# Graph attention with one leading neighbour: where the products of W stand among the projections

## The chip, the cores and the metric

The kernel runs on one core of a Trainium2 chip. The metric is the device time of one execution in microseconds (us), the median of several runs. Its engines are named as the profile names them: PE (TensorE matmul), PEld (its weight loads), DVE (VectorE), ACT (ScalarE), POOL (GpSimd) and SP (SyncE, which here only issues transfers). Each takes its instructions in the order in which the program gives them.

## The reference

The computation is one graph attention layer with four heads, a residual and a layer norm. x is 4096x512, adj 4096x4096, W 512x2048 (four heads of 512 columns) and a 4x1024x1, all float32.

```
ht = (h @ W).reshape(N, N_HEADS, N_HIDDEN).transpose(1, 0, 2)
src = jnp.einsum('hnd,hd->hn', ht, a[:, :N_HIDDEN, 0])
dst = jnp.einsum('hnd,hd->hn', ht, a[:, N_HIDDEN:, 0])
e = leaky_relu(src[:, :, None] + dst[:, None, :], 0.01) + adj_mat[None]
att = softmax(e, axis=-1)
h_prime = einsum('hij,hjd->hid', att, ht)
x = _layernorm(x + h_prime.mean(axis=0), axis=-1)
```

The adjacency holds weights of up to 1e9 and is added to scores of ordinary size. In a row whose largest adjacency entry leads the second by more than the scores can make up, the softmax is 1 at that column and 0 elsewhere. Then the layer gives x[i] + x[col(i)] @ mean over heads of W, followed by the norm.

## The kernel before, in words

`leading_rows` computes this short form for all rows, and a bound that tells whether it holds. `general`, the full attention, follows only where the bound fails; with the inputs here it does not run. So all that is profiled is `leading_rows`, lines 66 to 369.

The 4096 rows are worked in 32 blocks of 128 rows. The loop variable t counts 32 steps, and each step works on several blocks at different stages:

- **Adjacency.** SP loads a block of adj (128x4096, 2 MB) into one of six buffers; step t issues the load of block t+5, so the load waits until the block that used the buffer has been reduced. x is loaded in eight groups of four blocks into the tile `hold`, at steps given by the table `x_at`. W is first held in the slots of `hold` that the last four groups of x take over later, so those loads also wait for the products that read W.
- **Search.** DVE takes the maxima of segments of 64 columns in two halves (`segment_maxima(t, 0)` and `(t, 1)`, line 151). `find_segment(t)` finds the best segment and POOL gathers it from memory (`lead`, line 166). Two steps later `find_column(t-2)` finds the column in it, between the two halves, and POOL gathers that row of x (`y`, line 182; four buffers).
- **Projection.** At step t `project(t-3)` opens a sum in PSUM (`o`) with the residual, as identity times the block of x (line 191), turns y by four transposes into `tp` (line 194), has ACT copy them to `yt` (line 196), and adds four products of yt with `w_sum`, the mean of W over heads (line 198).
- **Norm.** `stats(t-4)` has ACT sum o and its squares (lines 208 and 210). At each even step from 6 on, `rstd` turns the sums of blocks t-6 and t-5 into scale and shift: a square root on ACT (line 213), then a reciprocal and a product on DVE (lines 214 and 215). `finish` applies them on ACT (line 219).
- **Bound.** It needs the products of W with both halves of a: W has sixteen 128x512 pieces, and `head_vector(kb, h)` turns one by four transposes (line 255), copies it on ACT (line 257) and forms four narrow products, two columns wide, into `pv` (line 259). The table `vectors_at` gives the steps: four pieces each at steps 1 and 2, one each at steps 3 to 10. `head_norms` follows at step 11. `row_norm` sums squares of x on ACT, and `bound` puts it together in three parts at steps 27 to 29.

After the loop come the last two columns, the last pairs' norms, the stores of the output by SP, `test` (the check of the bound, with one product on PE at line 307) and the projections of blocks 29 to 31. The order on every engine is the order of these calls, written by hand. In float32 the profile shows each matmul as two instructions, so four products of 512 columns are listed as x8.

Of the kernel before, what the change touches and what calls it, by code (L numbers as in the profile page):

```python
# [9 lines left out]
F32 = mybir.dt.float32  # L10
# [9 lines left out]
P = 128  # L20
# [45 lines left out]
def leading_rows(ctx, tc, x, adj, W, a, out, ident, v, n_bad, any_bad):  # L66
# [91 lines left out]
    def find_segment(ib):  # L158
        seg = seg_of.pop(ib)
        nc.vector.max(out=top[:, ib, :], in_=seg)  # L160
        at = small.tile([P, 8], U32, name="at")
        nc.vector.max_index(at, top[:, ib, :], seg)
        row = small.tile([P, 1], U32, name="row")
        nc.vector.tensor_tensor(row, at[:, 0:1], first[:, ib : ib + 1], op=OP.add)  # L164
        lead = small.tile([P, E], F32, name="lead")
        nc.gpsimd.indirect_dma_start(  # L166
            out=lead, out_offset=None, in_=adj_segs,
            in_offset=bass.IndirectOffsetOnAxis(ap=row[:, :1], axis=0),
        )
        at_of[ib], lead_of[ib] = at, lead  # L170
# [14 lines left out]
        )  # L185
        y_t[ib] = y

    def project(ib):
        y = y_t.pop(ib)
        o = psum.tile([P, D], F32, name="o")  # L190
        nc.tensor.matmul(o, ident, hold[:, ib, :], start=True, stop=False)  # L191
        tp = psum.tile([P, KB, P], F32, name="tp", bufs=2)
        for kb in range(KB):
            nc.tensor.transpose(tp[:, kb, :], y[:, ts(kb, P)], ident)  # L194
        yt = rows.tile([P, KB, P], F32, name="yt")
        nc.scalar.copy(yt, tp)  # L196
        for kb in range(KB):
            nc.tensor.matmul(o, yt[:, kb, :], w_sum[:, kb, :], start=False, stop=(kb == KB - 1))  # L198
        o_ps[ib] = o

    def row_norm(ib):
        sq = rows.tile([P, D], F32, name="sq")
# [9 lines left out]
    def rstd(i):  # L212
        nc.scalar.activation(sd[:, i], sd[:, i], AF.Sqrt, bias=eps, scale=1.0 / D)  # L213
        nc.vector.reciprocal(sd[:, i], sd[:, i])  # L214
        nc.vector.tensor_mul(nm[:, i], nm[:, i], sd[:, i])  # L215
# [35 lines left out]
    def head_vector(kb, h):  # L251

        tp = psum.tile([P, KB, P], F32, name="tp", bufs=2)
        for k in range(KB):
            nc.tensor.transpose(tp[:, k, :], hold[:, w_at + kb * H + h, ts(k, P)], ident)  # L255
        wt = rows.tile([P, KB, P], F32, name="wt")
        nc.scalar.copy(wt, tp)  # L257
        for k in range(KB):
            nc.tensor.matmul(  # L259
                pv[:, kb, h : 2 * H : H], wt[:, k, :], at_d[:, k, h : 2 * H : H],  # L260
                start=(k == 0), stop=(k == KB - 1),
            )

    def head_norms():
        nc.vector.tensor_copy(v, pv)
        vv = once.tile([P, KB, 2 * H], F32, name="vv")
        nc.vector.tensor_mul(vv, v, v)
        pn = psum.tile([P, KB, 2 * H], F32, name="px", bufs=1)
        nc.tensor.matmul(pn, ones, vv, start=True, stop=True)
        n2 = once.tile([P, 2 * H], F32, name="n2")  # L270
        nc.vector.tensor_reduce(n2, pn.rearrange("p k c -> p c k"), axis=AX.X, op=OP.add)
        nc.scalar.activation(n2, n2, AF.Sqrt)
        both = once.tile([P, H], F32, name="both")
        nc.vector.tensor_add(both, n2[:, :H], n2[:, H:])
        nc.vector.tensor_reduce(vn, both, axis=AX.X, op=OP.max)
# [34 lines left out]
        nc.vector.tensor_reduce(total, pg, axis=AX.X, op=OP.add)  # L310
        nc.vector.tensor_scalar(any_bad, total, -1.0, float(N), op0=OP.mult, op1=OP.add)

    x_at = {1: 1, 3: 2, 6: 3, 12: 4, 14: 5, 17: 6, 20: 7}
    norms_at = {t: [t - 2] for t in range(2, 18)}
    for k in range(8):
        norms_at[18 + k] = [16 + 2 * k, 17 + 2 * k]
    vectors = [(kb, h) for kb in range(KB) for h in range(H)]
    vectors_at = {1: 4, 2: 4, **{t: 1 for t in range(3, 11)}}
    COLUMN, PROJECT, STATS, FINISH = 2, 3, 4, 6

    for t in range(NB):
        if t in x_at:
            load_x(x_at[t])
        load_adj(t + AHEAD)
        segment_maxima(t, 0)
        if t >= COLUMN:
            find_column(t - COLUMN)
        if t >= FINISH and t % 2 == 0:
# [9 lines left out]
        if t == 11:  # L338
            head_norms()
        if t >= PROJECT:  # L340
            project(t - PROJECT)
        if t >= FINISH and t % 2 == 0:
# [6 lines left out]
        if 27 <= t <= 29:  # L349
            bound(t - 27)  # L350

    find_column(NB - 2)
    find_column(NB - 1)
# [246 lines left out]
```

## Time and profile before

| | us |
|---|---|
| median of 3 runs (lowest, highest) | 283.46 (280.98, 283.83) |
| the profiled execution | 282.4 |
| its span, first to last instruction | 280.5 |
| PE busy | 220.3 (79%) |
| DVE busy | 192.1 (68%) |
| ACT busy | 120.7 (43%) |
| POOL busy | 61.8 (22%) |

The kernel moves 97.75 MB, 89.15 read and 8.39 written, at a mean of 348 GB/s over the span. The mean granted clock of TensorE is 0.921 of full speed. The profiled execution took 1.9 us more than its span, which is what lies around the first and last instruction. A share of busy time is an average over stages with different limits, so the stages are read apart below: by slices of the span, by who waited for whom, and by the order of time. In the rows of a timeline the first number is the start in us from the start of the span, the second the length; what stands in brackets at the end is how long the engine was idle before it and who released it. In rows of the chain of work that ended last, the name is followed by xcount.

### The profile page before, as it was taken

What the parts mean: (1) busy time and instruction counts of PE and PEld (TensorE: products, weight loads), DVE (VectorE), ACT (ScalarE), POOL (GpSimd) and SP (SyncE); (2) the same over time, 40 slices, a digit from 0 to 9 for tenths busy, and PEclk for the clock granted to TensorE, in tenths of its full rate; (3) what the DMA queues carried; (4) which work ended last, traced back from release to release, by engine and by line L of the source; (5) the groups of instructions that cost most, each with busy time, mean ns of one, the idle gap of its engine ahead of it and who ended that gap; (6) DMA issues with size and microseconds to landing.
All of it is one profiled execution on the core that took longest, in us unless ns stands there. A gap on an engine that the chain in (4) does not pass through costs nothing.

```text
span 280.5 us, 2442 instructions
## 1 busy us (share of the span) xinstructions
PE 220.3 (79%) x683; PEld 112.6 (40%) x684; DVE 192.1 (68%) x381; ACT 120.7 (43%) x295; POOL 61.8 (22%) x75
## 2 busy tenths in 40 slices
PE   0389877778888888889987879887999789888980
PEld 0134666654444444434433333433444334343430
DVE  2524878840029695888999999599879999983011
ACT  1010211211465455365453735674566434465540
POOL 1101123310002222122332332232322322232000
PEclk9999755559999999999999997999899979999997
DMA  7999999999999979499999999999999999415121
GB/s 232 436 416 425 418 425 393 430 400 435 430 409 402 388 289 408 154 416 409 409 426 421 408 418 426 407 418 428 420 355 361 329 408 407 152 42 162 67 101 59
DMA packets 18147, 97.75 MB, mean 348 GB/s; under 512 B 1992, under 2 KB 1992, under 8 KB 13776
## 3 DMA queue, kind: packets, MB, share of 16 engines
q1 hardware_dynamic: 14384, 87.82, 77.9%
q0 software_dynamic: 3584, 9.44, 9.2%
q10 hardware_dynamic: 160, 0.28, 0.3%
q8 instruction: 7, 0.11, 0.2%
q14 instruction: 12, 0.10, 0.1%
HBM read 89.15 MB, written 8.39 MB: 348 GB/s over the span
## 4 chain that ended last, share of the span: by engine, by line
PE 43%; DMA 19%; DVE 18%; ACT 12%; issue 5%; ACTq 0%; POOLq 0%
PE o L198 19%; DVE seg L151 13%; DMA y<-in_x_dram,col 11%; PE pv L259 8%; DMA hold<-in_L_gnn_W_dram 6%; PE o L191 5%; ACT yt L196 4%; PE tp L255 4%; PE tp L194 3%; ACT wt L257 3%; PE o L238 3%; ACT sq L210 2%; DMA adj_t<-in_adj_dram 2%; ACT sq L203 2%; ACT sq L208 1%
## 5 line engine op out<-in xcount | busy, mean ns | idle before, releaser
L151 DVE TENSOR_REDUCE seg<-adj_t 128x32 f32<-128x2048 f32 (+1 forms) x68 | 146.2, 2153 | 22.9 <-DMA adj_t<-in_adj_dram 22.8
L198 PE MATMUL o<-w_sum,yt 128*128 128x512 f32 x256 | 123.4, 627 | 21.6 <-ACT yt L196 21.6
L198 PEld LDWEIGHTS o<-w_sum,yt 128*128 128x128 f32 x256 | 47.8, 197 | 78.5 <-issue 49.1
L196 ACT COPY yt<-tp 128x512 f32<-128x512 f32 x32 | 18.7, 585 | 86.0 <-PE tp L194 86.0
L166 POOL DMA_INDIRECT lead<-in_adj_dram,row x32 | 30.3, 948 | 107.8 <-DVE row L164 99.7
L182 POOL DMA_INDIRECT y<-in_x_dram,col x32 | 30.2, 944 | 85.7 <-issue 62.7
L214 DVE RECIPROCAL sd<-sd 128x2 f32<-128x2 f32 (+1 forms) x17 | 2.8, 163 | 48.7 <-ACT sd L213 48.6
L191 PE MATMUL o<-hold,ident 128*128 128x512 f32 x64 | 34.6, 623 | 0.0
L259 PE MATMUL pv<-at_d,wt 128*128 128x2 f32 x128 | 23.4, 304 | 11.3 <-ACT wt L257 11.3
L259 PEld LDWEIGHTS pv<-at_d,wt 128*128 128x128 f32 x128 | 22.0, 259 | 16.3 <-ACT wt L257 16.3
L238 PE MATMUL o<-hold,ident 128*128 128x512 f32 x32 | 15.6, 646 | 13.1 <-DMA hold<-in_L_gnn_W_dram 13.1
L194 PEld LDWEIGHTS tp<-ident,y 128*128 128x128 f32 x128 | 15.8, 143 | 25.2 <-issue 25.0
L194 PE MATMUL tp<-ident,y 128*128 128x128 f32 x128 | 19.9, 279 | 5.9 <-DMA y<-in_x_dram,col 5.9
L257 ACT COPY wt<-tp 128x512 f32<-128x512 f32 x16 | 9.4, 586 | 34.6 <-PE tp L255 34.6
L219 ACT ACTIVATE hold<-o,nm,sd 128x512 f32<-128x512 f32 x31 | 22.7, 780 | 3.0 <-DVE nm L215 3.0
L210 ACT ACTIVATE sq<-o,nm 128x512 f32<-128x512 f32 x31 | 21.3, 687 | 1.0
L203 ACT ACTIVATE sq<-hold 128x512 f32<-128x512 f32 x32 | 19.7, 619 | 0.0
L208 ACT ACTIVATE sq<-o 128x512 f32<-128x512 f32 x31 | 18.7, 603 | 0.0
L191 PEld LDWEIGHTS o<-hold,ident 128*128 128x128 f32 x64 | 11.5, 195 | 10.0 <-issue 9.9
L238 PEld LDWEIGHTS o<-hold,ident 128*128 128x128 f32 x32 | 6.5, 209 | 21.1 <-issue 18.9
L255 PE MATMUL tp<-ident,hold 128*128 128x128 f32 x64 | 13.3, 346 | 0.0
L239 ACT ACTIVATE w_sum<-o 128x512 f32<-128x512 f32 x4 | 2.4, 597 | 24.1 <-PE o L238 24.1
(66 smaller groups left out, 94.3 us busy)
## 6 DMA issues: line engine op xcount, KB each, us to landing
adj_t<-in_adj_dram SPq DMA_DIRECT2D x30, 2048.0 KB, 12.0
hold<-in_x_dram SPq DMA_DIRECT2D x8, 1024.0 KB, 15.8
out_dram<-hold SPq DMA_DIRECT2D x7, 1024.0 KB, 14.3
adj_t<-in_adj_dram SPq DMA_DIRECT2D x8, 512.0 KB, 6.5
hold<-in_L_gnn_W_dram SPq DMA_DIRECT2D x4, 1024.0 KB, 10.6
lead<-in_adj_dram,row POOLq DMA_INDIRECT x32, 6.4
y<-in_x_dram,col POOLq DMA_INDIRECT x32, 7.2
out_dram<-hold SPq DMA_DIRECT2D x1, 512.0 KB, 2.8
```

What stands on the lines that cost most here:

```text
L151: nc.vector.tensor_reduce(seg_of[ib][:, ts(k, S // n)], adj_t[ib][:, ts(k, N // n)].rearrange("p (s e) -> p s e", e=E), axis=AX.X, op=OP.max,)
L166: nc.gpsimd.indirect_dma_start(out=lead, out_offset=None, in_=adj_segs, in_offset=bass.IndirectOffsetOnAxis(ap=row[:, :1], axis=0),)
L182: nc.gpsimd.indirect_dma_start(out=y, out_offset=None, in_=x, in_offset=bass.IndirectOffsetOnAxis(ap=col[:, :1], axis=0),)
L191: nc.tensor.matmul(o, ident, hold[:, ib, :], start=True, stop=False)
L194: nc.tensor.transpose(tp[:, kb, :], y[:, ts(kb, P)], ident)
L196: nc.scalar.copy(yt, tp)
L198: nc.tensor.matmul(o, yt[:, kb, :], w_sum[:, kb, :], start=False, stop=(kb == KB - 1))
L203: nc.scalar.activation(sq, hold[:, ib, :], AF.Square, accum_out=xx[:, ib : ib + 1])
L210: nc.scalar.activation(sq, o, AF.Square, bias=nm[:, i], accum_out=sd[:, i])
L238: nc.tensor.matmul(o, ident, hold[:, w_at + kb * H + h, :], start=(h == 0), stop=(h == H - 1))
L255: nc.tensor.transpose(tp[:, k, :], hold[:, w_at + kb * H + h, ts(k, P)], ident)
L259: nc.tensor.matmul(pv[:, kb, h : 2 * H : H], wt[:, k, :], at_d[:, k, h : 2 * H : H], start=(k == 0), stop=(k == KB - 1),)
```

## The change

`project` now turns y first and computes the residual after the transposes. `head_vector` is split: `turn_w` does the transposes and the copy, and the rest does the four narrow products. From step 3 on, the W piece of a step is turned ahead of `project`, and its products are given to `project`, which sets them between the residual and the four wide products. The sixteen pieces spread over steps 1 to 14: two each at steps 1 and 2, one each at steps 3 to 14. Only the last block, `wait=True`, keeps its residual ahead of its transposes.

Four more things move. `rstd` stands after both halves of the segment maxima and after `find_segment`, where it stood between the halves. The loads of x move by a step or two (`x_at`). `head_norms` moves from step 11 to 16, and `row_norm` of the last blocks from steps 18 to 25 to steps 20 to 27. `bound` moves from the end of steps 27 to 29 to ahead of `project` at steps 28 to 30. No operation is added or removed.

```diff
-    def project(ib):
+    def project(ib, between=(), wait=False):
+        o = o_ps[ib] = psum.tile([P, D], F32, name="o")
+        def residual():
+            nc.tensor.matmul(o, ident, hold[:, ib, :], start=True, stop=False)
+        if wait:
+            residual()
         y = y_t.pop(ib)
-        o = psum.tile([P, D], F32, name="o")
-        nc.tensor.matmul(o, ident, hold[:, ib, :], start=True, stop=False)
         tp = psum.tile([P, KB, P], F32, name="tp", bufs=2)
         for kb in range(KB):
             nc.tensor.transpose(tp[:, kb, :], y[:, ts(kb, P)], ident)
         yt = rows.tile([P, KB, P], F32, name="yt")
         nc.scalar.copy(yt, tp)
+        if not wait:
+            residual()
+        for some in between:
+            head_vector(*some)
         for kb in range(KB):
             nc.tensor.matmul(o, yt[:, kb, :], w_sum[:, kb, :], start=False, stop=(kb == KB - 1))
...
-    x_at = {1: 1, 3: 2, 6: 3, 12: 4, 14: 5, 17: 6, 20: 7}
+    x_at = {1: 1, 4: 2, 8: 3, 11: 4, 14: 5, 18: 6, 21: 7}
...
-    vectors_at = {1: 4, 2: 4, **{t: 1 for t in range(3, 11)}}
+    vectors_at = {t: 2 if t < 3 else 1 for t in range(1, 15)}
...
-        if t >= FINISH and t % 2 == 0:
-            rstd(slice(t - FINISH, t - FINISH + 2))
         segment_maxima(t, 1)
         find_segment(t)
+        pair = t >= FINISH and t % 2 == 0
+        if pair:
+            rstd(slice(t - FINISH, t - FINISH + 2))
...
-        for _ in range(vectors_at.get(t, 0)):
-            head_vector(*vectors.pop(0))
+        turned = [(*vectors[0], turn_w(*vectors.pop(0))) for _ in range(vectors_at.get(t, 0))]
...
         if t >= PROJECT:
-            project(t - PROJECT)
+            project(t - PROJECT, turned)
+        else:
+            for some in turned:
+                head_vector(*some)
...
     for ib in range(NB - PROJECT, NB):
-        project(ib)
+        project(ib, wait=(ib == NB - 1))
```

On PE, the rows from the first products of W to the end of the first block's projection read before:

```order
L255 MATMUL tp<-ident,hold 128x128 x4
L259 MATMUL pv<-at_d,wt 128x2 x4
L255 MATMUL tp<-ident,hold 128x128 x4
L259 MATMUL pv<-at_d,wt 128x2 x4
L255 MATMUL tp<-ident,hold 128x128 x4
L259 MATMUL pv<-at_d,wt 128x2 x4
L191 MATMUL o<-hold,ident 128x512
L194 MATMUL tp<-ident,y 128x128 x4
L198 MATMUL o<-w_sum,yt 128x512 x4
```

These are the last three of nine pieces of W ahead of block 0 (tp turned W, pv its narrow products), then block 0's residual, its transposes and its wide products. In the changed kernel, whose lines are numbered anew, all that stands there is:

```order
L263 MATMUL tp<-ident,hold 128x128 x8
L271 MATMUL pv<-at_d,wt 128x2 x8
L263 MATMUL tp<-ident,hold 128x128 x8
L271 MATMUL pv<-at_d,wt 128x2 x8
L263 MATMUL tp<-ident,hold 128x128 x4
L200 MATMUL tp<-ident,y 128x128 x4
L193 MATMUL o<-hold,ident 128x512
L271 MATMUL pv<-at_d,wt 128x2 x4
L208 MATMUL o<-w_sum,yt 128x512 x4
```

Nine pieces ahead of block 0's wide products have become five: two pairs, and a fifth whose narrow products stand behind the residual.

On DVE, the rows of step 6, the first with `rstd`, read before:

```order
L151 TENSOR_REDUCE seg<-adj_t 128x32
L174 MAX inner<-lead 128x8
L176 MAX_INDEX within<-inner,lead 128x8
L178 SCALAR_TENSOR_TENSOR col<-at,within 128x1
L214 RECIPROCAL sd<-sd 128x2
L215 TENSOR_TENSOR nm<-nm,sd 128x2
L151 TENSOR_REDUCE seg<-adj_t 128x32
L160 MAX top<-seg 128x8
L162 MAX_INDEX at<-top,seg 128x8
L164 TENSOR_TENSOR row<-at,first 128x1
```

and in the changed kernel:

```order
L151 TENSOR_REDUCE seg<-adj_t 128x32
L174 MAX inner<-lead 128x8
L176 MAX_INDEX within<-inner,lead 128x8
L178 SCALAR_TENSOR_TENSOR col<-at,within 128x1
L151 TENSOR_REDUCE seg<-adj_t 128x32
L160 MAX top<-seg 128x8
L162 MAX_INDEX at<-top,seg 128x8
L164 TENSOR_TENSOR row<-at,first 128x1
L223 RECIPROCAL sd<-sd 128x2
L224 TENSOR_TENSOR nm<-nm,sd 128x2
```

The reciprocal, which waits for ACT's square root, has moved behind the second half of the maxima and the search of the segment.

More of the change, by code (lines that the diff above doesn't have):

```diff
@@ L249, in turn_a, with turn_w @@
         nc.scalar.copy(at_d, tp[:, :, : 2 * H])
-    def head_vector(kb, h):
+    def turn_w(kb, h):
         tp = psum.tile([P, KB, P], F32, name="tp", bufs=2)
@@ L257, in head_vector @@
         nc.scalar.copy(wt, tp)
+        return wt
+    def head_vector(kb, h, wt):
         for k in range(KB):
@@ L311, in test @@
         nc.vector.tensor_scalar(any_bad, total, -1.0, float(N), op0=OP.mult, op1=OP.add)
-    x_at = {1: 1, 3: 2, 6: 3, 12: 4, 14: 5, 17: 6, 20: 7}
+    x_at = {1: 1, 4: 2, 8: 3, 11: 4, 14: 5, 18: 6, 21: 7}
     norms_at = {t: [t - 2] for t in range(2, 18)}
     for k in range(8):
-        norms_at[18 + k] = [16 + 2 * k, 17 + 2 * k]
+        norms_at[20 + k] = [16 + 2 * k, 17 + 2 * k]
     vectors = [(kb, h) for kb in range(KB) for h in range(H)]
-    vectors_at = {1: 4, 2: 4, **{t: 1 for t in range(3, 11)}}
+    vectors_at = {t: 2 if t < 3 else 1 for t in range(1, 15)}
     COLUMN, PROJECT, STATS, FINISH = 2, 3, 4, 6
@@ L335, in leading_rows @@
             turn_a()
-        for _ in range(vectors_at.get(t, 0)):
-            head_vector(*vectors.pop(0))
-        if t == 11:
+        turned = [(*vectors[0], turn_w(*vectors.pop(0))) for _ in range(vectors_at.get(t, 0))]
+        if t == 16:
             head_norms()
+        if 28 <= t <= 30:
+            bound(t - 28)
         if t >= PROJECT:
-            project(t - PROJECT)
-        if t >= FINISH and t % 2 == 0:
+            project(t - PROJECT, turned)
+        else:
+            for some in turned:
+                head_vector(*some)
+        if pair:
             finish(t - FINISH)
@@ L348, in leading_rows @@
             row_norm(ib)
-        if 27 <= t <= 29:
-            bound(t - 27)
     find_column(NB - 2)
```

1 line of the change is left out of this document (removed).

## The prediction

> **What bounds the kernel now.** I read the page's slices first, then who waited for whom on DVE, then the order of time on PE and DVE, then the tail. In the slices each digit is a fortieth of the span, 7.0 us:
>
> ```profile
> DVE  2524878840029695888999999599879999983011
> PEclk9999755559999999999999997999899979999997
> DMA  7999999999999979499999999999999999415121
> ```
>
> DVE stands still from slice 9 to slice 12, just behind a stretch in which PE has half its clock, and DMA has its holes only later, in slices 15 and 17. The wait table, with total, count and longest, and the order of time on DVE name what it waited for:
>
> ```profile
> DVE sd L214 <- ACT sd L213: 48.6, 10, 22.0
> 57.60 2.29 DVE L151 TENSOR_REDUCE seg<-adj_t 128x32 f32<-128x2048 f32 x1 [2.43 <-DMA adj_t<-in_adj_dram]
> 82.51 0.17 DVE L214 RECIPROCAL sd<-sd 128x2 f32<-128x2 f32 x1 [21.96 <-ACT sd L213]
> 96.97 0.17 DVE L214 RECIPROCAL sd<-sd 128x2 f32<-128x2 f32 x1 [2.43 <-ACT sd L213]
> 112.86 0.17 DVE L214 RECIPROCAL sd<-sd 128x2 f32<-128x2 f32 x1 [3.84 <-ACT sd L213]
> 178.18 0.17 DVE L214 RECIPROCAL sd<-sd 128x2 f32<-128x2 f32 x1 [3.04 <-ACT sd L213]
> 204.63 0.17 DVE L214 RECIPROCAL sd<-sd 128x2 f32<-128x2 f32 x1 [2.40 <-ACT sd L213]
> 241.55 0.17 DVE L214 RECIPROCAL sd<-sd 128x2 f32<-128x2 f32 x1 [0.46 <-ACT sd L213]
> ```
>
> These are six of seven such waits inside the loop, the first and the last among them; the seventh is 0.5, together 34.7 us. The rest of the 48.6 is behind the loop, where DVE is not needed. Queued on DVE behind the reciprocal of step 6 are the second half of block 6's maxima and with it the release of its buffer. Why the square root is late stands in the chain of work that ended last, which is PE there (start, length, what):
>
> ```profile
> 29.11 0.60 PE tp L255 x4
> 55.97 0.97 PE tp L255 x4
> 57.66 1.87 PE pv L259 x8
> 59.53 1.91 PE o L191 x2
> 67.84 1.05 PE pv L259 x8
> 68.89 0.97 PE o L191 x2
> 69.86 0.45 PE tp L194 x4
> 70.33 0.59 ACT yt L196
> 70.97 3.70 PE o L198 x8
> ```
>
> From 29.1 to 59.5 PE does nine pieces of W, most at half clock (0.97 for a turn, 1.87 for its products), each waiting for ACT's copy. Block 0 begins at 59.5, although its y had been fetched long before: POOL's row and the landing times of the gathers (min, median, max) are
>
> ```profile
> 32.26 0.95 POOL L182 DMA_INDIRECT y<-in_x_dram,col  x1 [6.66 <-DVE col L178]
> DMA to landing us min/median/max: 3.3/7.2/10.1
> DMA to landing us min/median/max: 2.4/6.4/7.8
> ```
>
> the second row for y, the third for the segments (lead). So y of block 0 was there by 32.3 + 7.2 = 39.5, at the latest 42.4. Block 0 is 17 to 20 us late, and DVE's 22 us follow from it.
>
> **What DVE costs without its waits.** Two starts of maxima, of blocks 14 and 16, and the last of block 31:
>
> ```profile
> 136.22 2.28 DVE L151 TENSOR_REDUCE seg<-adj_t 128x32 f32<-128x2048 f32 x1
> 148.17 2.28 DVE L151 TENSOR_REDUCE seg<-adj_t 128x32 f32<-128x2048 f32 x1
> 247.72 2.34 DVE L151 TENSOR_REDUCE seg<-adj_t 128x16 f32<-128x1024 f32 x2
> ```
>
> One block costs (148.17 - 136.22)/2 = 5.98 us, reciprocals included. Call T the end of block 31's maxima: 247.72 + 2.34 = 250.1 now. From 57.60 to 250.1 are 192.5 us, of which 34.7 are the waits, so without them T would be 57.6 + 157.8 = 215.4.
>
> **What PE costs after the change.** The four pieces of steps 1 and 2 take at most 4 x (0.97 + 1.87) = 11.4 us from 29.1, so they end by 40.5; five pieces less stand ahead of block 0. I start block 0 at 41, between the bounds 39.5 and 42.4. It begins on a cold clock: a turn and the residual cost 0.5 and 0.9 more by the half-clock rows, 1.5 together. From then a block with a piece of W costs 0.45 + 0.45 + 0.97 + 1.05 + 3.70 = 6.62, since both copies of 0.59 now lie under the residual and the narrow products (before, 7.8 with both copies in the open); a block without one costs 5.1. DVE and DMA deliver one y in about 6, so in twelve blocks PE falls behind by at most 12 x 0.6 = 7 us if nothing else holds the blocks back, and from block 12 it gains 0.9 a block.
>
> **Whether DVE still waits for the square root.** The rows of one pass, from the gather to the reciprocal, in steps 14 to 16, and ACT's one loading of a table, are
>
> ```profile
> 139.92 7.61 DMA y<-in_x_dram,col
> 147.66 0.64 PE tp L194 x4
> 151.14 0.18 DVE sd L214
> L213 ACT ACT_TABLE_LOAD x1 | 1.3, 1283 | 0.0
> ```
>
> From the start of y's transposes to the reciprocal are 3.5 us. At step 6 the reciprocal needs the sums of block 1, which ACT takes behind the copy of block 2's yt: block 2 is turned at 41 + 1.5 + 2 x 6.62 + 0.45 = 56.2, plus 3.5 and 1.3 gives 61.0, plus 0.6 for the added W copy 61.6. DVE's place is now behind the segment of step 6, at 57.6 + 5.6 = 63.2 (5.98 less the pair itself), so the 22 us go. In the later steps block 16 (start 148.17) found its root at 151.1, 3.0 into the step; the new place is 2.9 further on. That margin covers a PE or a gather up to 2.9 late, which are the waits of 3.04 and 2.40; if the cover were gone, one us late at each of the 13 pairs costs at most 13.
>
> **What else moves.** `row_norm`, later by two steps, changes no sum on ACT, which is busy for 43% of the span. `bound` now stands ahead of a projection on PE, so that block waits for DVE's short reduction behind the segment. Its y lands about there anyway, at (139.92 + 7.61 - 136.22) = 11.3 behind the start of the step that found its column, 5.3 into the next, where DVE gets to the reduction at 5.6. That is 0.5, with a square root between 1.2, on blocks where PE gains 0.9 each: nothing, bounded by 1.2. `head_norms` holds DVE while PE and ACT answer, at step 16 as it did at step 11; up to 2 us more if PE is late, which falls into DVE's waits for adj below.
>
> **What is late next: DMA.** The page's counts and two stretches (busy times left of the clock, then DMA share and GB/s):
>
> ```profile
> q0 software_dynamic: 3584, 9.44, 9.2%
> adj_t<-in_adj_dram SPq DMA_DIRECT2D x30, 2048.0 KB, 12.0
> hold<-in_x_dram SPq DMA_DIRECT2D x8, 1024.0 KB, 15.8
> 7.00:98.00 91.00, 72.27 (x262) 44.64 (x263) 47.29 (x83) 25.25 (x56) 14.33 (x15) 0.83 1.01 416
> 203.00:224.00 21.00, 18.39 (x50) 8.09 (x48) 18.79 (x35) 12.76 (x35) 6.12 (x7) 1.00 0.95 350
> ```
>
> A block of adj with its gathers is 2.097 + 9.44/32 = 2.39 MB, at 416 GB/s 5.75 us; a group of x is 1.05 MB, 2.52 us. The change moves these loads on SP but takes none away. Groups 2 to 7 now stand behind block 8 and up to just ahead of block 26. From block 6 (landed at 57.6) block 26 lands at 57.6 + 20 x 5.75 + 6 x 2.52 = 187.7. DVE could start it at 57.6 + 20 x 5.98 = 177.2, so it waits for DMA about 10 us in this stretch, and a PE 7 us late is hidden there. From block 26 the loads are faster than DVE: five blocks at 5.98, 0.7 for the bound's short pieces, 5.25 for block 31. T = 187.7 + 29.9 + 0.7 + 5.3 = 223.6, 26.5 less than now.
>
> **The tail.** Now it takes 280.5 - 250.1 = 30.4 us from T:
>
> ```profile
> 251.12 2.37 DMA lead<-in_adj_dram,row
> 255.56 0.22 PE px L307 x2
> 261.65 0.86 PE o L191 x2
> 273.03 0.71 DVE st L224
> ```
>
> PE comes to the product of the test (px) 5.5 after T, then three blocks of 0.86 + 0.45 + 0.66 (copy in the open) + 3.70 = 5.67. Two of them lose the 0.66; the last keeps it, its residual being first. That is 29.1. But px stands ahead of the three blocks on PE and waits for the last gather, which now takes 2.37 on a nearly idle DMA. After the change the loads end at 187.7 + 5 x 5.75 = 216.5 and six stores, 6.3 MB, follow for 15 us, past T. The nearest row for a gather on busy DMA is the median 6.4, so 4.0 more: 33.1, between 29.1 and, at the longest landing 7.8, 34.5. End: 223.6 + 33.1 = 256.7 of span; with the 1.9 around it 258.6. The profiled execution, 282.4, stands 1.1 below the median of the runs, as much as runs differ; I leave that, and take 258.5.
>
> **A rule on the clock.** One row shows what a clock dip costs:
>
> ```profile
> 168.03 5.40 PE o L198 x8
> ```
>
> It is 1.7 more than 3.70, behind a wait for y of about 1.5. The Trainium skill, "TensorE: Matmul & The Clock Gate", section "HAM oscillation — how this bites in real kernels", says that each idle gap longer than its window of 3.4 us makes the next products start at half clock; the row shows a dip after a shorter gap, so here the row decides. By the rule only block 0 would start cold, by the row some later blocks too; both stay within the margins above, and the sum is the same.
>
> **The rivals.** (1) DMA does not hold back DVE, because groups of x land in time that DMA has left: T is 215.4, and with a tail of 29.1 to 33.1 the time is 246.4 to 250.4. For it: in slices 10 to 12 DMA ran on while DVE stood still. Against: the bytes have to pass, at 416 over 91 us. Chance 0.15. (2) The wait stays in part: PE at 6.62 a block with dips of 1.7, or gathers of 10.1, make the root later than the margin, and half of the 34.7 stays: T is 215.4 + 17.3 = 232.7, the time 267.7. Chance 0.13. (3) DMA falls to 350 GB/s, as from 203 to 224: block 26 lands at 57.6 + 130.1 x 416/350 = 212.2, the time is 283.1, no change. Against it: at 204.6 DVE waited and released no buffer, so SP had nothing to issue. Chance 0.05. The Trainium skill, "DMA: Bandwidth & Descriptors", section "Where 436 GB/s comes from", says that for transfers from HBM the HBM side binds at about 358 GB/s a core; the same sum gives about 280 by that figure. The 416 above, over 91 us, speaks against it. (4) Slower: PE keeps half its clock through the twelve mixed blocks, as in slices 6 to 9. A block then costs 2 x 0.97 + 1.91 + 1.87 + 7.40 (twice 3.70, an estimate) = 13.1, twelve end at 41 + 157 = 198, twenty more at 5.1 end at 300, and with the 7.5 from the last product to the end of the span and 1.9 the time is 309. It decides from about 10.8 a block on. Against it: with the same mixture PE had full clock from 63 on. Chance 0.05. (5) Early waits go, but another, which I don't see, takes their place and the time is that of before: 0.02.
>
> **How the numbers follow.** The forecast has what is left, 0.60, with its own range 253 to 264 (tail 29.1 to 34.5, dips and DMA 2% either way). The range must take in rival 1 and rival 2: 246 to 270 leaves out about 0.15. One per cent, 2.8 us, is about what a measurement here tells from no change. Faster by more: 0.60 + 0.15 + 0.13 = 0.88; within: 0.07; slower: 0.05.
>
> **What would show it.** In the changed kernel's profile block 0's first transposes start between 39 and 43; the reciprocal of step 6 waits under 1 us; clock near 1.0 from 45 on; waits of DVE for adj after step 8 of some 10 us in total; DMA without holes to 215; T near 224; lead of block 31 landing in 5 to 8. I am wrong in the main if the reciprocals still wait 10 us or more in all, and wrong in the size if DVE hardly waits for adj (then rival 1) or PE's blocks cost over 7.5.

## The result, and the profile after

The changed kernel takes **259.47 us** (median of 4 runs, 258.17 to 260.56) against 283.39 for the kernel before beside it (4 runs, 280.98 to 283.83). The ratio is 0.917, with a 95% interval of 0.910 to 0.924. The profiled execution took 259.82 us, its span is 258.0, and the mean granted clock is 0.942 (0.921 before). A run over 1.5% above the fastest of its kernel is left out of the ratios, here and below: single runs of the kernel before, and one of the four of kernel e12 (276.36), whose other three have a median of 269.51.

The slices of the changed kernel's page, each a fortieth of the span, 6.45 us, answer to those shown of before:

```profile
DVE  2608479959979997997889999899799999821011
PEclk9999956999999999999959999999999799995997
DMA  6999999999999999999999999999999999996031
```

Two things are gone: the low digits of DVE in slices 9 to 12, and the long stretch of half clock in slices 6 to 9, of which two slices are left (PEclk 5 and 6). The single 5 in slice 21 is `head_norms`, for whose input PE waits 3.1 us. The holes in DMA's row are gone too: it is at 9 from slice 2 to slice 36. So the transfers now run without a break to beyond the end of the maxima. The windows of the changed kernel say how fast (busy times of PE, PEld, DVE, ACT and POOL, then clock, DMA share and GB/s):

```profile
28.00:45.00 17.00, 14.00 (x75) 11.00 (x74) 13.61 (x21) 5.24 (x12) 3.77 (x4) 0.70 1.03 422
45.00:60.00 15.00, 13.93 (x57) 7.89 (x56) 11.63 (x22) 7.33 (x17) 3.77 (x4) 1.00 1.02 414
98.00:216.00 118.00, 99.53 (x298) 46.30 (x297) 107.10 (x209) 65.40 (x169) 34.29 (x37) 0.96 1.01 417
```

The stretch from 28 to 63 had a clock of 0.56 before. Now the clock is back at 1.00 from 45 to 60.

The changed kernel's table of who waited for whom (total, count, longest) has DVE's waits:

```profile
DVE seg L151 <- DMA adj_t<-in_adj_dram: 30.9, 14, 7.9
DVE sd L223 <- ACT sd L222: 14.9, 3, 6.6
DVE inner L174 <- DMA lead<-in_adj_dram,row: 5.3, 1, 5.3
```

The waits for the square root (now lines 222 and 223) went from 48.6 us in ten to 14.9 in three, and these three stand behind the loop. In the order of time on the changed kernel's DVE, the reciprocal of step 6, the first and the last but one of the seven waits for adj behind step 8, block 31's last maxima, and the gather that DVE waits for behind them:

```profile
63.55 0.16 DVE L223 RECIPROCAL sd<-sd 128x2 f32<-128x2 f32 x1
77.35 2.29 DVE L151 TENSOR_REDUCE seg<-adj_t 128x32 f32<-128x2048 f32 x1 [1.51 <-DMA adj_t<-in_adj_dram]
187.48 2.29 DVE L151 TENSOR_REDUCE seg<-adj_t 128x32 f32<-128x2048 f32 x1 [1.82 <-DMA adj_t<-in_adj_dram]
221.25 2.34 DVE L151 TENSOR_REDUCE seg<-adj_t 128x16 f32<-128x1024 f32 x2
230.32 0.23 DVE L174 MAX8 inner<-lead 128x8 f32<-128x64 f32 x1 [5.29 <-DMA lead<-in_adj_dram,row]
```

The first row has no bracket: the reciprocal that waited 21.96 us waits for nothing. The last maxima end at 221.25 + 2.34 = 223.59, which is the prediction's T; before it was 250.1. The tail from there to the end of the span is 258.0 - 223.6 = 34.4, four more than the 30.4 before. So 26.5 us are gained up to T, 4.0 are given back behind it, and the span is 22.5 shorter.

On PE, the first projections and the beginning of the tail of the changed kernel:

```profile
40.83 1.09 PE L200 MATMUL tp<-ident,y 128*128 128x128 f32 x4 [2.55 <-DMA y<-in_x_dram,col]
...
49.47 0.63 PE L200 MATMUL tp<-ident,y 128*128 128x128 f32 x4 [1.07 <-DMA y<-in_x_dram,col]
49.94 1.02 PE L193 MATMUL o<-hold,ident 128*128 128x512 f32 x2
50.80 0.95 PE L271 MATMUL pv<-at_d,wt 128*128 128x2 f32 x8
51.61 3.68 PE L208 MATMUL o<-w_sum,yt 128*128 128x512 f32 x8
55.13 0.60 PE L263 MATMUL tp<-ident,hold 128*128 128x128 f32 x4
55.56 0.60 PE L200 MATMUL tp<-ident,y 128*128 128x128 f32 x4
...
69.12 0.63 PE L200 MATMUL tp<-ident,y 128*128 128x128 f32 x4 [1.27 <-DMA y<-in_x_dram,col]
...
232.37 0.27 PE L319 MATMUL px<-gap,ones 128*1 128x32 f32 x2 [5.05 <-DVE gap L317]
232.56 1.12 PE L200 MATMUL tp<-ident,y 128*128 128x128 f32 x4
233.47 1.92 PE L193 MATMUL o<-hold,ident 128*128 128x512 f32 x2
235.18 5.05 PE L208 MATMUL o<-w_sum,yt 128*128 128x512 f32 x8
```

Block 0 starts at 40.83, where it started at 59.5, and it is PE that waits for its y. The five rows from 49.47 on are block 1 with its piece of W: transposes, residual, narrow products, wide products and the turn of the next piece follow each other without a gap. In the tail PE stands for 5.05 us before the product of the test (px). Block 29 behind it then runs on a cold clock: its residual takes 1.92 and its products 5.05, where a warm block takes 1.02 and 3.68.

### The profile page after: what moved, and what is told of

Read it like the earlier page. It is cut to its first block, busy times and chain, and to the rows that moved or that the text cites. A ratio compares the mean times of both kernels' runs of the same rounds, so it can differ in the third digit from the quotient of the medians.

```text
span 258.0 us, 2438 instructions
## 1 busy us (share of the span) xinstructions
PE 207.3 (80%) x683; PEld 105.6 (41%) x684; DVE 191.9 (74%) x381; ACT 120.5 (47%) x295; POOL 61.8 (24%) x75
## 5 line engine op out<-in xcount | busy, mean ns | idle before, releaser
L208 PE MATMUL o<-w_sum,yt 128*128 128x512 f32 x256 | 121.7, 619 | 0.7 <-ACT yt L202 0.7
L200 PE MATMUL tp<-ident,y 128*128 128x128 f32 x128 | 21.2, 291 | 20.4 <-DMA y<-in_x_dram,col 20.4
L193 PE MATMUL o<-hold,ident 128*128 128x512 f32 x64 | 35.9, 645 | 0.0
L200 PEld LDWEIGHTS tp<-ident,y 128*128 128x128 f32 x128 | 15.1, 149 | 33.5 <-issue 30.0
L247 PE MATMUL o<-hold,ident 128*128 128x512 f32 x32 | 16.4, 670 | 12.6 <-DMA hold<-in_L_gnn_W_dram 12.6
L219 ACT ACTIVATE sq<-o,nm 128x512 f32<-128x512 f32 x31 | 21.3, 687 | 1.0
L271 PEld LDWEIGHTS pv<-at_d,wt 128*128 128x128 f32 x128 | 18.2, 210 | 7.2 <-issue 4.8
L271 PE MATMUL pv<-at_d,wt 128*128 128x2 f32 x128 | 17.0, 257 | 0.5 <-ACT wt L265 0.5
L247 PEld LDWEIGHTS o<-hold,ident 128*128 128x128 f32 x32 | 6.7, 216 | 21.1 <-issue 19.6
L223 DVE RECIPROCAL sd<-sd 128x2 f32<-128x2 f32 (+1 forms) x17 | 2.7, 158 | 14.9 <-ACT sd L222 14.9
L174 DVE MAX8 inner<-lead 128x8 f32<-128x64 f32 x32 | 7.0, 218 | 5.3 <-DMA lead<-in_adj_dram,row 5.3
L193 PEld LDWEIGHTS o<-hold,ident 128*128 128x128 f32 x64 | 10.5, 204 | 0.5 <-issue 0.5
## 6 DMA issues: line engine op xcount, KB each, us to landing
adj_t<-in_adj_dram SPq DMA_DIRECT2D x30, 2048.0 KB, 33.1
```

The source lines that it names most:

```text
L219: nc.scalar.activation(sq, o, AF.Square, bias=nm[:, i], accum_out=sd[:, i])
L247: nc.tensor.matmul(o, ident, hold[:, w_at + kb * H + h, :], start=(h == 0), stop=(h == H - 1))
L271: nc.tensor.matmul(pv[:, kb, h : 2 * H : H], wt[:, k, :], at_d[:, k, h : 2 * H : H], start=(k == 0), stop=(k == KB - 1),)
```

## The experiments

Twelve kernels were run, each beside the kernel before, whose medians there were 283.41, 282.09 and 283.6. In the table T is the end of block 31's maxima, the tail is what the span has behind it, and "in the loop" sums DVE's waits for the square root up to step 30.

| kernel | edit | median us (lowest, highest) | ratio, 95% interval | in the loop | T | tail |
|---|---|---|---|---|---|---|
| before | | 283.39 (280.98, 283.83) | | 34.7 | 250.1 | 30.4 |
| changed | | 259.47 (258.17, 260.56) | 0.917, 0.910 to 0.924 | 0 | 223.6 | 34.4 |
| e1 | before, reciprocal behind the search | 275.58 (275.06, 277.85) | 0.973, 0.968 to 0.979 | 27.2 | 245.5 | 30.6 |
| e2 | before, pieces spread | 275.92 (274.66, 276.52) | 0.974, 0.967 to 0.980 | 28.4 | 244.0 | 30.5 |
| e11 | before, inner order alone | 262.72 (260.98, 263.0) | 0.927, 0.918 to 0.935 | 16.4 | 232.2 | 29.0 |
| e12 | before, the first eight pieces in groups | 270.86 (268.19, 276.36) | 0.955, 0.941 to 0.969 | 21.3 | 237.2 | 30.5 |
| e3 | changed, inner order undone | 271.71 (271.01, 272.08) | 0.960, 0.954 to 0.965 | 22.3 | 238.4 | 31.5 |
| e4 | changed, reciprocal back between the halves | 262.02 (261.25, 262.8) | 0.926, 0.920 to 0.932 | 9.3 | 226.6 | 33.2 |
| e5 | changed, eight pieces first | 259.42 (259.23, 259.8) | 0.920, 0.913 to 0.927 | 0 | 223.9 | 33.7 |
| e6 | changed, without four groups of x | 251.44 (249.9, 252.18) | 0.891, 0.883 to 0.898 | 0 | 217.9 | 31.5 |
| e8 | changed, x at the steps of before | 259.77 (259.31, 260.59) | 0.920, 0.914 to 0.927 | 0 | 224.1 | 34.7 |
| e7 | changed, test ahead of block 31 | 259.27 (258.57, 259.73) | 0.919, 0.912 to 0.926 | 0 | 223.8 | 33.5 |
| e10 | changed, norm of blocks 26 and 27 earlier | 259.80 (259.01, 260.42) | 0.918, 0.910 to 0.925 | 0 | 224.1 | 34.6 |
| e9 | changed, both of the last two | 253.55 (252.83, 253.56) | 0.896, 0.888 to 0.903 | 0 | 223.8 | 28.0 |

The theory was that of the prediction: DVE's waits for the square root go, a DMA without a break then sets T, and the last gather sets the tail. The first five runs ask which part of the change removes the waits.

**e1: the place of the reciprocal alone.**

```diff
-        if t >= FINISH and t % 2 == 0:
-            rstd(slice(t - FINISH, t - FINISH + 2))
         segment_maxima(t, 1)
         find_segment(t)
+        if t >= FINISH and t % 2 == 0:
+            rstd(slice(t - FINISH, t - FINISH + 2))
```

> The kernel before with one part of the change: the pair's norm stands behind the search of the segment. My theory (PE delivers late, so DVE waits wherever the reciprocal stands): block 0 on PE still begins near 59.5, the reciprocal of step 6 still waits, 19 us in place of 22; steps 8 to 12 wait 2 to 4 as before; the three waits behind step 12 (5.9 in sum) go. T, the end of block 31's maxima, 250 - 9 = 241; time 272 to 276. Rival (the place of the reciprocal was what held DVE): the waits go nearly all, time 262 or less.

Measured 275.58, 7.8 less than before. The row of step 6 on its DVE:

```profile
84.78 0.17 DVE L214 RECIPROCAL sd<-sd 128x2 f32<-128x2 f32 x1 [20.93 <-ACT sd L213]
```

The wait at step 6 is 20.93, since block 0 is as late as before. Waits of 2.43 and 3.85 follow at steps 8 and 10, and none later in the loop. So the place alone covers the small late roots, as expected. T came out at 245.5 where 241 was expected; the time lay in its range. Of the 4.5, 1.9 are the wait at step 6, expected at 19, and 2.6 a wait that was not expected: `head_norms` at step 11 holds DVE for 3.12 us, waiting for PE, where it held it for 0.56 before. A PE that is 20 us late can't be covered by a place 2.9 further on.

**e2: the spread of the pieces alone.**

```diff
-    vectors_at = {1: 4, 2: 4, **{t: 1 for t in range(3, 11)}}
+    vectors_at = {t: 2 if t < 3 else 1 for t in range(1, 15)}
...
-        if t == 11:
+        if t == 16:
             head_norms()
```

> The kernel before with the sixteen pieces of W spread over steps 1 to 14 and their norms at step 16, each piece still turned and multiplied in one go ahead of its block, residual first, reciprocals between the halves. My theory: block 0 begins near 44 and the wait of step 6 falls to 7, but PE needs 8.0 us for each of twelve blocks, so DVE waits some 3 to 4 us at each of steps 8 to 16. T 241 to 247, time 271 to 279, 275 the likeliest. Rival (the early start is all of the gain): T near 225, time 258 to 262.

Measured 275.92, as expected. The wait at step 6 falls to 8.24, but eight more follow, the first five of them 2.43, 3.85, 3.85, 3.85 and 1.57: in the serial order PE doesn't make up its delay while the pieces last.

**e3: the changed kernel without its inner order.** Each piece is turned and multiplied at once, and each residual stands ahead of the transposes, so that the copies are in the open.

```diff
-        turned = [(*vectors[0], turn_w(*vectors.pop(0))) for _ in range(vectors_at.get(t, 0))]
+        for _ in range(vectors_at.get(t, 0)):
+            kb, h = vectors.pop(0)
+            head_vector(kb, h, turn_w(kb, h))
...
-            project(t - PROJECT, turned)
-        else:
-            for some in turned:
-                head_vector(*some)
+            project(t - PROJECT, wait=True)
...
-        project(ib, wait=(ib == NB - 1))
+        project(ib, wait=True)
```

> The changed kernel with the inner order of PE undone: each piece of W in one go ahead of its block, the residual ahead of the transposes, so that PE waits for both copies; spread, place of the reciprocal and loads as changed. My theory: PE at 8.0 us a mixed block becomes the bound up to block 11, reciprocals wait about 4 us at steps 6 to 16, T 236 to 239, time 270 to 273, so the interleaving is worth some 12 us. Rival (DMA bounds the changed kernel so much that PE's copies are hidden): time 259 to 262.

Measured 271.71: the inner order is worth 12.2 us of the 23.9, with the two other parts in place. The first pass shows why (DVE of e3):

```profile
70.56 0.17 DVE L223 RECIPROCAL sd<-sd 128x2 f32<-128x2 f32 x1 [6.74 <-ACT sd L222]
```

Step 6 waits 6.74, though only five pieces stand ahead of block 0 and the reciprocal is at its new place. Block 0 starts on PE at 45.25 here, not at 40.83.

**e4: the changed kernel with the reciprocal back between the halves.**

```diff
-        segment_maxima(t, 1)
-        find_segment(t)
         pair = t >= FINISH and t % 2 == 0
         if pair:
             rstd(slice(t - FINISH, t - FINISH + 2))
+        segment_maxima(t, 1)
+        find_segment(t)
```

> The changed kernel with the reciprocal back between the halves of the maxima. My theory: in the changed kernel's profile the roots are ready within 0 to 1.2 us of the old place, and up to step 24 what they cost falls into DVE's waits for adj, so T rises by 1 to 3 and the time is 259 to 263. Rival (the place matters by itself): waits of 2 to 3 at each of 13 pairs, time 270 or more.

Measured 262.02, as expected. Seven waits of 0.42 to 1.86 come back, 9.3 us in all, and T moves by only 3.0, because DVE waits less for adj in their place (1.3 us behind step 8 instead of 8.1). The place is worth 2.5 us.

**e5: eight pieces ahead of block 0 again, all else as changed.**

```diff
-    vectors_at = {t: 2 if t < 3 else 1 for t in range(1, 15)}
+    vectors_at = {1: 4, 2: 4, **{t: 1 for t in range(3, 11)}}
```

> The changed kernel with the spread undone: four pieces of W at each of steps 1 and 2, one each at steps 3 to 10. My theory: block 0 begins near 54.5, the reciprocal of step 6 waits 10 to 13 us, the later ones 0 to 2, and since DMA runs on through that wait a part of it is given back; T 226 to 231, time 262 to 267. Rival (all of the first wait comes back): T 235, time 271.

A miss. Measured 259.42: without the spread nothing is lost. In the order of time on the PE of e5, from the first turn to block 0:

```profile
30.49 1.15 PE L263 MATMUL tp<-ident,hold 128*128 128x128 f32 x8 [0.18 <-ACT wt L265]
31.48 3.65 PE L271 MATMUL pv<-at_d,wt 128*128 128x2 f32 x32
34.99 3.65 PE L263 MATMUL tp<-ident,hold 128*128 128x128 f32 x16
38.49 3.82 PE L271 MATMUL pv<-at_d,wt 128*128 128x2 f32 x32
43.05 1.06 PE L200 MATMUL tp<-ident,y 128*128 128x128 f32 x4
```

The inner order does more than set products between a residual and a projection: where a step has four pieces and no block, it turns all four first. PE then waits for one copy, 0.18 us, in the first four pieces. Before, each piece waited 0.68 or 0.73, as in this row of its PE:

```profile
36.34 1.87 PE L259 MATMUL pv<-at_d,wt 128*128 128x2 f32 x8 [0.73 <-ACT wt L257]
```

The eight pieces take from 29.2 to 42.2, 13.0 us; before, the first eight took from 29.0 to 55.8, 26.8 us. Of the 13.8 us between them, the eight waits for a copy (two of 0.68, six of 0.73, less the 0.18) are 5.6. The other 8.2 are the clock: nearly all the pieces of before ran at half clock, 1.09 for a turn and 1.87 for its products. Block 0 starts at 43.05, only 2.2 us later than with the spread. The window that both kernels fill with pieces, of before and then of e5:

```profile
28.80:41.00 12.20, 9.38 (x50) 7.93 (x50) 9.91 (x16) 3.02 (x6) 2.83 (x3) 0.61 1.03 423
```

```profile
28.80:41.00 12.20, 12.02 (x93) 11.18 (x92) 9.81 (x16) 5.26 (x11) 2.80 (x3) 0.86 1.04 426
```

PE does 93 matmuls in it instead of 50, hardly idle and at a clock of 0.86 instead of 0.61. The prediction had priced the pieces by the half-clock rows of the serial order, and credited the spread with what the grouping does.

**e11: the inner order alone, in the kernel before.** Its tables, its place of the reciprocal and everything else stay. The edit is what the diff of the change shows of `project`, `turn_w`, `turned` and `wait`, and nothing more:

```diff
-        for _ in range(vectors_at.get(t, 0)):
-            head_vector(*vectors.pop(0))
+        turned = [(*vectors[0], turn_w(*vectors.pop(0))) for _ in range(vectors_at.get(t, 0))]
...
-            project(t - PROJECT)
+            project(t - PROJECT, turned)
+        else:
+            for some in turned:
+                head_vector(*some)
```

> The kernel before with the inner order of PE alone (pieces of a step turned first, products behind the residual, residual behind the transposes); pieces at the steps of before, the reciprocal between the halves, loads and bound as before. My theory now: the inner order carries the change, block 0 begins near 43, the reciprocals wait some 8 us in all, T 225 to 229, time 261 to 265. Rival (the parts add up): 268 to 274.

Measured 262.72, in the range: the inner order alone brings 20.7 of the 23.9 us. T was missed, 232.2 where 225 to 229 was expected, and so were its steps: block 0 starts at 45.68 instead of 43, and the reciprocals wait 16.4 instead of 8. That the time fits all the same is luck, because the tail is only 29.0: DMA is nearly free by then (share 0.27 from 232 to 236, where the changed kernel has 1.05 from 224 to 230), and the last gather is waited for 2.05 instead of 5.29. In the order of time on the PE of e11:

```profile
31.48 3.63 PE L271 MATMUL pv<-at_d,wt 128*128 128x2 f32 x32
36.34 1.97 PE L263 MATMUL tp<-ident,hold 128*128 128x128 f32 x8 [0.29 <-issue]
38.11 6.83 PE L271 MATMUL pv<-at_d,wt 128*128 128x2 f32 x32
45.68 1.06 PE L200 MATMUL tp<-ident,y 128*128 128x128 f32 x4
```

The second group's products take 6.83 where e5 has 3.82 for the same instructions in the same order: here they ran at about half clock, behind a gap of 0.29. Up to 35 us the two traces read alike. What made the clock fall here and not there was not settled. With its later T, e11 is only 0.7 us above e4, which has the spread, the other tables and the other place of `bound` besides: what e4 gains up to T, 5.6, it gives back in a tail longer by 4.2, and the rest of the difference lies in the spread of the runs. `row_norm`, `head_norms` and `bound` have no run of their own; these 0.7 us of time are what they and the spread bring together on top of the inner order.

**e12: only the grouping of the first eight pieces, in the kernel before.** The four pieces of a step are turned ahead of their products, for which `head_vector` is split as in the change; residuals and later pieces keep the serial order.

```diff
-        for _ in range(vectors_at.get(t, 0)):
-            head_vector(*vectors.pop(0))
+        turned = [(*vectors[0], turn_w(*vectors.pop(0))) for _ in range(vectors_at.get(t, 0))]
+        for some in turned:
+            head_vector(*some)
```

> The kernel before with one edit: the four pieces of steps 1 and 2 are all turned ahead of their products, so PE waits for one copy of four; from step 3 on each piece and block as before. My theory: the eight pieces take 13 us as in the kernel with eight first, block 0 begins near 44, but eight mixed blocks at 8.0 leave waits of 6 at step 6 and 2 to 4 at steps 8 to 12; T 233 to 238, time 265 to 270. Rival (the early groups are all): 260 to 263.

Measured 270.86 with a wide spread (268.19 to 276.36), 0.9 above the expected range; without the highest run the median is 269.51, in the range, and that is also the profiled execution. T is in its range, but block 0 starts at 47.31 where 44 was expected. The first products of the eight pieces on its PE, and the row of step 6 on its DVE:

```profile
31.50 5.23 PE L262 MATMUL pv<-at_d,wt 128*128 128x2 f32 x32
70.43 0.17 DVE L214 RECIPROCAL sd<-sd 128x2 f32<-128x2 f32 x1 [9.67 <-ACT sd L213]
```

The grouping alone takes the wait at step 6 from 21.96 to 9.67 and gives 12.5 of the 20.7 us of the inner order, 13.9 without the highest run. The rest, 8.1 or 6.8, is the difference to e11, whose residual and narrow products stand over the copies in the later steps. The same 32 products take 5.23 here and 3.65 in e5, though on PE the two traces read alike up to their start, with 0.18 as the only wait in the pieces: so the clock can fall without the gap of e11.

**e6: does DMA set T?** The changed kernel without the loads of groups 4 to 7 of x, so the residuals and norms of blocks 16 to 31 read what was left in `hold`; this leaves out a part of the computation.

```diff
-        if t in x_at:
+        if t in x_at and x_at[t] < 4:
             load_x(x_at[t])
```

> The changed kernel without the loads of x groups 4 to 7 (blocks 16 to 31 then use what W left in their place; that part of the result is left out). It takes 4.2 MB, 10 us of DMA, from ahead of block 26 and nothing from any engine. My theory (DMA sets T in the changed kernel): block 26 no longer waits, DVE's 8 us of waits for adj behind step 8 shrink to about 3, those of the first three groups; T 216 to 218, loads end sooner and the tail is 31 to 34, time 250 to 254. Rival (DVE's own work or PE sets the pace): no change, 258 to 260.

Measured 251.44, in the range. Behind step 8, two waits for adj are left on its DVE where the changed kernel has seven:

```profile
77.47 2.29 DVE L151 TENSOR_REDUCE seg<-adj_t 128x32 f32<-128x2048 f32 x1 [1.55 <-DMA adj_t<-in_adj_dram]
102.70 2.29 DVE L151 TENSOR_REDUCE seg<-adj_t 128x32 f32<-128x2048 f32 x1 [1.25 <-DMA adj_t<-in_adj_dram]
```

None is left after 103 us. T falls by 5.7 to 217.9, which is the 215.4 that the prediction gave for DVE without waits and these 2.8, within 0.3. The four groups are 4 x 2.52 = 10.1 us of DMA; 5.7 of them reach T, and then DVE is the bound. So DMA sets T in the changed kernel, by the bytes that have to pass.

**e8: the loads of x at the steps of before.**

```diff
-    x_at = {1: 1, 4: 2, 8: 3, 11: 4, 14: 5, 18: 6, 21: 7}
+    x_at = {1: 1, 3: 2, 6: 3, 12: 4, 14: 5, 17: 6, 20: 7}
```

> The changed kernel with x loaded at the steps of the kernel before. My theory: each group is moved by one or two places among loads that all have to pass ahead of block 26, so T moves by under 0.5 and the time is within 1.5 us of 259.5. Rival (the table matters, as x3 then stands ahead of block 11 where DVE has just caught up with DMA): 262 or more.

Measured 259.77, no change: the same bytes in another order.

The last three runs ask about the tail.

**e7: the test ahead of block 31 only.**

```diff
-    test()
     for ib in range(NB - PROJECT, NB):
+        if ib == NB - 1:
+            test()
         project(ib, wait=(ib == NB - 1))
```

> The changed kernel with the test ahead of block 31's projection in place of ahead of block 29's, so PE's wait of 5.05 for the test's product no longer holds three blocks. My theory (the test's place and the gather behind it set the tail): block 29 starts when its y lands, 2 to 4 us sooner, and loses its clock dip of 1.4 on the wide products and 1.4 on the rest; T stays 223.6, tail 28 to 30, time 253 to 256. Rival (stores and the gathers of y set the tail): within 1 us of 259.5.

A miss. Measured 259.27, no change. PE no longer waits for the test, but in the order of time on the PE of e7 another wait stands there:

```profile
228.65 0.63 PE L200 MATMUL tp<-ident,y 128*128 128x128 f32 x4 [1.18 <-DMA y<-in_x_dram,col]
233.57 5.40 PE L208 MATMUL o<-w_sum,yt 128*128 128x512 f32 x8 [3.43 <-ACT yt L202]
```

Block 29 is turned at 228.65, but its copy comes late. ACT of e7 says why:

```profile
231.59 1.45 ACT L228 ACTIVATE hold<-o,nm,sd 128x512 f32<-128x512 f32 x2 [6.15 <-DVE nm L224]
232.93 0.58 ACT L202 COPY yt<-tp 128x512 f32<-128x512 f32 x1
```

The copy is queued on ACT behind `finish` of blocks 26 and 27, which waits for DVE's scale and shift, which are queued on DVE behind `find_column` of block 31, which waits for the last gather. So there are two ways from that gather to block 29, one through the test on PE and one through the norm on DVE and ACT, and they end close to each other: block 29's wide products start at 235.18 in the changed kernel, behind the first, and at 233.57 here, behind the second. The 1.6 us between them hardly show in the time.

**e10: the norm of blocks 26 and 27 ahead of the last column, the test where it was.**

```diff
     find_column(NB - 2)
-    find_column(NB - 1)
     rstd(slice(NB - FINISH, NB - FINISH + 2))
     finish(NB - FINISH)
     finish(NB - FINISH + 1)
+    find_column(NB - 1)
```

> The changed kernel with only the last pair's norm and finish ahead of the search of block 31's column; the test stays ahead of block 29. My theory: PE's wait of 5 us for the test's product stays, no gain, time 258.5 to 260.5. Rival (ACT's finish is the hold that counts): 253 to 256.

Measured 259.80, no change, as expected: PE waits 4.75 for the test again.

**e9: both edits.**

> The kernel with the late test, and besides the last pair's norm and finish (blocks 26 and 27) ahead of the search of block 31's column, so that neither PE's test product nor ACT's finish waits for block 31's gather. My theory (two holds lie side by side behind that gather, each hides the other): block 29's copy follows its transposes at once, its wide products start near 230 in place of 233.6, block 31 ends some 5 us sooner; span 251 to 253, time 253 to 256. Rival (gathers of y under the stores set the tail): 258 to 260.

Measured 253.55, as expected, and the fastest kernel that leaves nothing out: 5.9 us below the changed kernel, T unchanged at 223.8. On its PE:

```profile
228.71 0.63 PE L200 MATMUL tp<-ident,y 128*128 128x128 f32 x4 [1.24 <-DMA y<-in_x_dram,col]
230.04 3.68 PE L208 MATMUL o<-w_sum,yt 128*128 128x512 f32 x8
```

Block 29's products start at 230.04 and take 3.68: both the wait and the cold clock are gone. Either edit alone brings nothing that the runs can tell, both bring 5.9, because the two holds lie side by side and the later one counts.

## Why the prediction was right, point by point

The forecast of 258.5 was 1.0 below the median, and by its own steps:

- **Block 0 starts at 41.** Measured 40.83, waiting for its y, as the bound by the gather had it. PE's own term was too high: the four pieces end at 37.2 instead of 40.5, the turn of the fifth at 38.3, and then PE waits 2.55.
- **The 22 us of step 6 go.** Measured 0, and none of the loop's 34.7 is left. The new place has a margin for it: ACT has the root at 60.5 (61.6 in the sum) and DVE comes to it at 63.55 (63.2). e4, without that margin, waits 1.86 there; its block 0 also ran on a colder clock (6.25 for the wide products, 3.68 in the changed kernel).
- **DVE waits about 10 for adj instead.** Seven waits behind step 8, 8.07 together. Block 26 starts at 187.48, predicted 187.7; T is 223.6, predicted 223.6. That the bytes of x pass without room, which rival 1 denied, is shown by e6: without four groups of them T is 217.9.
- **A mixed block costs 6.62 on PE.** Mis-sized, with no effect on the time: from the transposes of block 1 at 49.47 to those of block 2 at 55.56 are 6.1, and PE waited for a y again at 69.12. From start to start the parts are 0.47, 0.86, 0.81, 3.52 and 0.43, where the sum had 0.45, 0.97, 1.05, 3.70 and 0.45: lengths whose ends overlap the next start. PE did not fall 7 us behind; the delay that the prediction hid under DMA's waits hardly arose.
- **The tail takes 33.1.** Measured 34.4, inside its range to 34.5, but put together differently. The last gather landed 5.7 after its issue, less than the 6.4 taken: px comes 8.8 behind T instead of 9.5. Block 29 then runs cold for 7.5 us (232.56 to 240.07) where 5.0 was summed, which the prediction did not have. That the total is only 1.3 off is in part luck: 0.7 less up to px, 2.5 more in block 29 and 0.5 less in the rest partly cancel. And px was named as the only hold of the three blocks; e7 and e10 show a second beside it.
- **Which part does it.** The prediction took block 0's earlier start from the spread, "five pieces less stand ahead of block 0", and priced the pieces by half-clock rows of the serial order. It is right that they are fewer, and e2 shows that this helps the serial order (8.24 at step 6 instead of 21.96). In the changed kernel it carries nothing: e5 has the same time without it, and e3, with the spread but in the serial order, starts block 0 at 45.25. What carries is the inner order. That step failed as a cause, though its number was right, and there it was luck: the y of block 0 sets the start.
- **The clock dip of 5.40.** The prediction read it as one behind a wait for y of about 1.5. The row before it on PE has a wait for y of 1.24, and the products wait another 0.68 for the copy. Nothing in the sum rests on this.

The parts don't add up: alone they bring 7.8 (e1), 7.5 (e2) and 20.7 (e11), 36 together, of 23.9. The last two shorten the same wait at step 6. e1 takes 1.0 from it and removes the small waits behind step 12, and where the inner order has made DVE catch up with DMA, most of these turn into waits for adj, as e4 shows. Behind all of them DMA sets a T which none of them moves.

The rivals: rival 1 (DMA hidden) is out by the waits and by e6. Rival 2 (half of the waits stay) is out for the changed kernel; e11 looks like it, with 16.4 us of waits. Rival 3 (DMA at 350 GB/s) and the figure of about 358 that the Trainium skill gives in "DMA: Bandwidth & Descriptors", section "Where 436 GB/s comes from", are out: 417 GB/s over 118 us. Rival 4 (half clock through the mixed blocks) is out: the clock was 1.00 from 45 to 60.

## What to carry to other kernels

Where an engine does several short pairs of work with a copy on another engine between them, turn all first and multiply all after: one copy is waited for instead of each. That was worth more here (12.5 us alone) than taking work out of the way (7.5 alone), though the larger part of what PE saved came with a higher clock, whose cause is open. Before crediting an edit, price its work in the order that the change gives it, not by rows of the order it replaces. When a wait is removed and the time stays, look for a second chain from the same late event: two holds side by side show a gain only when both are moved.

## What the runs showed of the hardware

- **The length of a gap alone doesn't tell whether the clock falls.** In the changed kernel, from 60 us to the end of the loop, PE's wide products behind waits for y of up to 2.25 us take 3.68; behind the one of 2.77 they take 4.87:

```profile
167.27 0.63 PE L200 MATMUL tp<-ident,y 128*128 128x128 f32 x4 [2.25 <-DMA y<-in_x_dram,col]
168.60 3.68 PE L208 MATMUL o<-w_sum,yt 128*128 128x512 f32 x8
...
199.66 0.63 PE L200 MATMUL tp<-ident,y 128*128 128x128 f32 x4 [2.77 <-DMA y<-in_x_dram,col]
201.41 4.87 PE L208 MATMUL o<-w_sum,yt 128*128 128x512 f32 x8
```

  In e5 the same block waits longer and its products take 3.68:

```profile
199.98 0.63 PE L200 MATMUL tp<-ident,y 128*128 128x128 f32 x4 [2.87 <-DMA y<-in_x_dram,col]
201.30 3.68 PE L208 MATMUL o<-w_sum,yt 128*128 128x512 f32 x8
```

  And before, a wait of 1.24 for y with one of 0.68 for the copy behind it was enough for 5.40. The Trainium skill, "TensorE: Matmul & The Clock Gate", section "HAM oscillation — how this bites in real kernels", speaks of gaps above 3.4 us; in the changed kernel 2.77 was enough, and in e5 2.87 was not.
- **A PE that is busy can be at half clock.** Before, the clock was 0.61 from 28.8 to 41 with PE busy for 77% and no gap above 0.73, and 0.50 from 45 to 60 with PE busy for 81%. From 28.8 to 41 it was higher with the pieces in groups, 0.86 (e5), 0.81 (e11) and 0.72 (e12), but these three have the same pieces in the same order there, and the clock fell at different places in them. What decides is open.
- **The gather at the end.** With the stores of the output behind the last loads it landed 5.7 us after its issue (DMA share 1.05 from 224 to 230.3), where the kernel before, on a DMA with little else to do (0.20 from 251 to 253.5), had 2.37.
